# Strided deal of W and proj, a VectorE transpose of the B rows, and G through DRAM, in a LoRA and expert-mixture kernel

## The chip, the cores and the metric

The kernel runs on one core of one Trainium2 chip. The metric is device time in microseconds (us), the median of three runs. A core has five engines that run their own instruction streams and meet at semaphores: TensorE (PE in the profile, its weight loads PEld), VectorE (DVE), ScalarE (ACT), GpSimd (POOL) and SyncE (SP), which here only issues transfers. ACT and POOL issue transfers as well. All transfers of a core run on the same 16 DMA engines. Everything is in 32-bit floats.

## The reference, cut to what matters

`x` is (8, 512, 2048): 8 batches of 512 tokens. A linear layer W with bias b and a per-batch LoRA pair (A, Bm, rank 16) makes a hidden vector; a router picks one of 8 experts for each token from it; the expert's rank-16 pair adds to x.

```python
def cond(x, adapter_mapping, W, b, lora_As, lora_Bs):      # SCALING = 2
    base_out = jnp.einsum('bti,oi->bto', x, W) + b
    A, Bm = lora_As[adapter_mapping], lora_Bs[adapter_mapping]
    lora_h = jnp.einsum('bti,bir->btr', x, A)
    return base_out + jnp.einsum('btr,bro->bto', lora_h, Bm) * SCALING

def ffn(x, route_w, A, Bw):                                # E = 8, R = 16
    logits = jnp.einsum('bsd,ed->bse', x, route_w)
    topk_v, topk_idx = jax.lax.top_k(logits, 1)
    route_weight = one_hot(topk_idx[..., 0], E) * topk_v
    h = jnp.einsum('bsd,erd->bser', x, A)
    return jnp.einsum('bser,eor->bso', route_weight[..., None] * h, Bw)

out = x + ffn(cond(x, itok, W, b, lora_As, lora_Bs), route_w, A, Bw)
```

Nothing needs the 2048-wide hidden vector itself: only its 136 products with `proj` (128 expert rows and 8 router rows) are used. So the kernel folds W into proj first (C = projT W, 2048 x 136), and adds to it for each batch the product A G, where G = 2 Bm proj. Then every token tile needs one product of x with a 2048 x 136 matrix, the routing, and one product with the experts' second matrix.

## The kernel before, in words

There is no scheduler. The order of each engine's instructions is that of the program text (`tc.manual_schedule()`), and the waits between engines are placed from the tiles that they read and write.

**First stage: the fold (lines 383 to 427, about the first 77 us).** W comes in 16 chunks of 128 rows by 2048 columns (1 MB each). `load_w(oc)` (line 99) starts one transfer on SP for chunk `oc`, whose partition p holds row 128 oc + p; there are four buffers, so chunk n + 4 is started when chunk n has been copied out. `load_pj(c0, c1)` (line 94) loads the matching rows of proj, some through ACT's queue, most through SP's. `chunk_w(oc)` (line 260) copies a chunk into two half tiles in another column order, one half on ACT and one on DVE (line 274). `fold_w(oc)` (line 280) runs 16 matmuls of 128 x 136 (line 285) into six PSUM banks, which collect over all 16 chunks. A matmul in 32-bit floats shows as two instructions in the trace. `fold_w` can run a function `within` after half of its matmuls. In the last chunk it adds each bank to the adapter product of batch 0 (line 296) and copies the bank to `c` (line 297).

Between the chunks stand the adapter steps:

- `load_adapters_b` (line 157, after chunk 4) computes row numbers on DVE, gathers the 128 B rows of the 8 batches into `ad_b` with an indirect transfer of POOL (line 167) and loads the bias, which comes as 128 rows of 16 numbers, with a plain one (line 173). `load_adapters_a` (line 175, after chunk 7) gathers the A rows (line 179).
- `turn_adapters(g)` (line 313) turns the B rows with 4 TensorE transposes for each of 4 groups (line 316) and an ACT copy (line 317) into `ad_bT`.
- `fold_bias` (line 304) multiplies the bias into proj on DVE; `project_bias` and `project_adapters` (lines 321 and 326, after chunk 11) make the constant `c0b` and G, which lands in `g_sb` (line 333), one row for each of the 8 x 16 ranks.
- `spread_g(ks)` (line 335) brings 32 rows of G into all four quadrants of 32 partitions with a TensorE product against a tile of repeated identities, `eyes` (line 339), and DVE writes it out twice, each time masked by `half` (line 348), into `g4`.
- `spread_a` copies the A rows into quadrants (`ad_q`, lines 207 and 209): 20 copies on POOL after chunk 8, 4 on ACT after chunk 11.
- `first_products` (line 374) forms A G for batch 0 in pieces (line 361), two PSUM banks at a time, and copies them to `m`.

**Second stage (from line 436).** The 32 token tiles pass through `heads` (16 matmuls of x against m, line 452), `route` on DVE, `turn_heads` and `delta` (the expert product, line 546), `add_delta` and a store. x is loaded in units of two tiles by `load_x(u)` (line 116). Before a unit can be used, its quadrants are moved by 16 copies, `shuffle` (line 242, shared between POOL and ACT), and turned by DVE, `turn_x` (line 220), in 32 x 32 blocks. Units 0, 1 and 2 are loaded within the first stage (lines 405, 414 and 415); unit 0 is moved there, 10 of its copies on POOL after the A copies and 6 on ACT, and unit 1's 11 POOL copies follow.

The order around the change is, at the end of the loop's body:

```python
        if oc == 11:
            ...
            nc.sync.dma_start(out=fb, in_=ffn_b)
            load_x(1)
            load_x(2)
            project_bias()
            project_adapters()
```

Of the kernel before, what the change touches and what calls it, by code (L numbers as in the profile page):

```python
# [18 lines left out]
def kernel(  # L19
# [27 lines left out]

    nc = tc.nc  # L50
    P = 128
    Q = 32
# [21 lines left out]
    qpool = ctx.enter_context(tc.tile_pool(name="qpool", bufs=2))  # L74
    tpool = ctx.enter_context(tc.tile_pool(name="tpool", bufs=3))
    small = ctx.enter_context(tc.tile_pool(name="small", bufs=2))
    wctx = ctx.enter_context(ExitStack())
    wpool = wctx.enter_context(tc.tile_pool(name="wpool", bufs=1))
    ps_s = ctx.enter_context(tc.tile_pool(name="ps_s", bufs=2, space=bass.MemoryType.PSUM))
# [9 lines left out]

    it_i = const.tile([P, B], I32, name="it_i")  # L90
    pj = wpool.tile([P, NO, NP], F32, name="pj")
    proj_v = proj.rearrange("(c p) e -> p c e", p=P)

    def load_pj(c0, c1, eng=nc.sync):
        eng.dma_start(out=pj[:, c0:c1, :], in_=proj_v[:, c0:c1, :])  # L95
# [2 lines left out]

    def load_w(oc):
        wt = wpool.tile([P, D], F32, tag="w", bufs=4, name=f"w_{oc}")  # L100
        nc.sync.dma_start(out=wt, in_=w[ts(oc, P), :])  # L101
        w_tiles.append(wt)

    load_pj(0, 1, nc.scalar)
    load_w(0)
    load_w(1)
    load_pj(3, 5)
    load_w(2)
    load_pj(5, 8)
    load_w(3)  # L110

    x_tiles = {}
# [12 lines left out]
    make_identity(nc, ident)  # L125

    nc.scalar.copy(warm_a[:, 1:2], warm_a[:, :1])
    load_pj(1, 3, nc.scalar)
    nc.scalar.dma_start(out=it_i, in_=itok.to_broadcast([P, B]))
    pm = ps_s.tile([P, P], F32, tag="s", name="pm")  # L130
    for _ in range(14):
        nc.tensor.matmul(pm, warm, warm, start=True, stop=True)

    own_i = const.tile([P, B], I32, name="own_i")
# [15 lines left out]
    ad_b = raw[:, 0, :]  # L150
    ad_ar = raw[:, 1, :]
    fb = const.tile([P, D], F32, name="fb")
    bias_o = const.tile([P, NO], F32, name="bias_o")

    brow_f = const.tile([P, 1], F32, name="brow_f")

    def load_adapters_b():

        it_f = const.tile([P, B], F32, name="it_f")
        nc.vector.tensor_scalar(it_f, it_i, float(R), None, ALU.mult)  # L160
        row_f = const.tile([P, B], F32, name="row_f")
        nc.vector.tensor_tensor(row_f, it_f, own, ALU.add)
        nc.vector.tensor_tensor(row_f, row_f, mask, ALU.mult)
        nc.vector.tensor_reduce(brow_f, row_f, AX.X, ALU.add)
        brow_i = const.tile([P, 1], I32, name="brow_i")
        nc.vector.tensor_copy(brow_i, brow_f)  # L166
        nc.gpsimd.indirect_dma_start(  # L167
            out=ad_b,
            out_offset=None,
            in_=cond_b,  # L170
            in_offset=bass.IndirectOffsetOnAxis(ap=brow_i, axis=0),
        )
        nc.gpsimd.dma_start(out=bias_o, in_=bias)

    def load_adapters_a():

# [27 lines left out]
    def spread_a(q, k, copy):  # L204
# [3 lines left out]
        if q < 2:  # L208
            copy(dst[:, 3:], src[:, ds(JC + 2 * q, 2)])

    ad_bT = tpool.tile([P, NJ, P], F32, tag="t", name="ad_bT")

    g4 = const.tile([P, B, NP], F32, name="g4")
# [4 lines left out]
    def turn(dst, src, h):  # L218
# [7 lines left out]
    eyes = const.tile([P, NQ, Q], F32, name="eyes")  # L226
    nc.vector.tensor_reduce(
        eyes[:, 0, :], ident.rearrange("p (q c) -> p c q", c=Q), AX.X, ALU.add
    )
    nc.vector.tensor_copy(eyes[:, 1:, :], eyes[:, :1, :].to_broadcast([P, NQ - 1, Q]))  # L230

    xq_tiles = {}
    moves = [(g, i) for i in range(NQ) for g in range(NQ)]
# [26 lines left out]
    def chunk_w(oc):  # L260
        copies = (nc.scalar.copy, nc.vector.tensor_copy)
        wv = [
            wpool.tile([P, HJ, P], F32, tag=f"wv{h}", bufs=2, name=f"wv{h}_{oc}")
            for h in range(2)
        ]
        wr = w_tiles[oc].rearrange("p (i j a) -> p j i a", i=NQ, a=Q)
        for h in range(2):
            wv_tiles[oc, h] = wv[h]
            dst = wv[h].rearrange("p j (i a) -> p j i a", a=Q)

            n = HJ // 2 if oc == 0 else HJ
            for k in range(HJ // n):
                copy = copies[1 - k] if oc == 0 else copies[h]
                copy(dst[:, ts(k, n)], wr[:, ds(h * HJ + k * n, n)])  # L274
        if oc + 4 < NO:
            if oc in (0, 1):
                load_pj(8 + 4 * oc, 12 + 4 * oc)
            load_w(oc + 4)

    def fold_w(oc, within=None):  # L280
# [29 lines left out]
                    bp, pj[:, j, :], bias_o[:, j : j + 1], bp, ALU.mult, ALU.add  # L310
                )

    def turn_adapters(g):
        pt = ps_s.tile([P, 4, P], F32, tag="s", name=f"pbT_{g}")
        for k in range(4):
            nc.tensor.transpose(pt[:, k, :], ad_b[:, ts(4 * g + k, P)], ident)  # L316
        nc.scalar.copy(ad_bT[:, ts(g, 4), :], pt)

    g_sb = wpool.tile([P, NP], F32, name="g_sb")

    def project_bias():
        pb = ps_s.tile([P, NP], F32, tag="s", name="pb")
# [9 lines left out]
            )  # L332
        nc.vector.tensor_scalar(g_sb, pg, COND_SCALING, None, ALU.mult)

    def spread_g(ks):

        for k in ks:
            pq = ps_s.tile([P, NP], F32, tag="s", name=f"pq_{k}")
            nc.tensor.matmul(  # L339
                pq,  # L340
                eyes[ts(k, Q)].rearrange("p q c -> p (q c)"),
                g_sb[ts(k, Q), :],
                start=True,
                stop=True,
                tile_position=(k * Q, 0),
            )
            for h in range(2):
                nc.vector.tensor_scalar(
                    g4[:, 2 * k + h, :], pq, half[:, h : h + 1], None, ALU.mult
                )  # L350


    pieces = [(0, 3 * q, 3, q) for q in range(NQ)] + [(1, 2 * q, 2, q) for q in range(2)]
# [17 lines left out]
        part, j0, nj, _ = pieces[z]  # L371
        return (t[part][:, ds(j0, nj), :] for t in (ms[b % 2], cs))

    def first_products(some, copy=nc.vector.tensor_copy):
        banks = {
            z: ps_s.tile([P, GRP, NP], F32, tag="s", name=f"pa_{z}") for z in some
        }
        adapter_products(0, some, banks)
        for z in some:
            m, _ = place(0, z)  # L380
            copy(m, banks[z][:, : pieces[z][2], :])

    chunk_w(0)
    for oc in range(NO):
        if oc + 1 < NO:
            chunk_w(oc + 1)
        fold_w(
            oc,
            {
                13: lambda: spread_g((2, 3)),  # L390
                14: lambda: first_products((2, 3)),
            }.get(oc),
        )
# [289 lines left out]
```

## Time and profile before

| | before |
|---|---|
| median of 3 runs | 326.51 us (326.45 to 326.69) |
| the profiled execution's own time | 326.17 us |
| its span | 324.4 us |
| PE busy | 318.7 us (98%) |
| DVE, ACT, POOL busy | 230.1, 185.4, 164.9 us |
| first matmul of the fold | 7.06 us |
| first matmul of the second stage (line 452) | 77.02 us in the chain |
| DMA share, 14.87 to 68.60 us | 1.00 to 1.02 |
| HBM read, written | 54.60 MB, 33.55 MB |

The span is the time from the first to the last instruction in the trace; the 1.8 us between it and the execution's own time lie outside. The chain of waits is followed back from the last instruction, so a stretch that it gives to PE is one in which PE itself was the limit. The DMA share is the mean busy share of the 16 DMA engines. A matmul's time in the list of groups covers its pipeline; in the chain, 32 instructions of line 285 (one chunk) take 3.71 us.

### The profile page before, as it was taken

How to read it: one execution, taken by the hardware profiler on the slowest of the kernel's cores; microseconds unless marked ns; L12 is line 12 of the kernel's file. 1: busy time of each engine (PE TensorE's matmuls, PEld its weight loads, DVE VectorE, ACT ScalarE, POOL GpSimd, SP SyncE). 2: the span in 40 equal slices, each digit the busy share in tenths (PEclk: the TensorE clock that was granted, in tenths of full speed). 3: DMA queues.
4: the chain of work that ended last, by engine and by line, in shares of the span. 5: the costliest groups of instructions: out<-in, count | busy, mean ns of one | idle time of the engine just before them, and what ended most of it. 6: DMA issues, size and time to landing. Idle time of an engine off the chain costs nothing.

```text
span 324.4 us, 5611 instructions
## 1 busy us (share of the span) xinstructions
PE 318.7 (98%) x2168; PEld 252.6 (78%) x2168; DVE 230.1 (71%) x408; ACT 185.4 (57%) x230; POOL 164.9 (51%) x180
## 2 busy tenths in 40 slices
PE   8999999999999999999999999999999999999994
PEld 8999999999776777777768677767676777766762
DVE  2123183468879788887887888788787887888864
ACT  3223247527958567748764976596567758770000
POOL 1002149998967676257717771946295357710000
PEclk9999999999999999999999999999999999999999
DMA  7999999953933385859395949585876759334437
GB/s 281 365 404 421 420 418 420 421 231 120 401 129 129 131 284 235 301 233 368 153 375 229 361 165 395 184 353 165 355 255 266 270 250 358 162 162 179 174 144 250
DMA packets 15306, 88.52 MB, mean 273 GB/s; under 512 B 1696, under 2 KB 4016, under 8 KB 4912
## 3 DMA queue, kind: packets, MB, share of 16 engines
q1 hardware_dynamic: 14112, 85.45, 67.2%
q0 software_dynamic: 320, 2.11, 1.6%
q10 hardware_dynamic: 848, 0.61, 0.6%
q8 instruction: 17, 0.28, 0.4%
q14 instruction: 9, 0.07, 0.1%
HBM read 54.60 MB, written 33.55 MB: 272 GB/s over the span
## 4 chain that ended last, share of the span: by engine, by line
PE 94%; DMA 4%; SPq 0%; ACT 0%; DVE 0%; issue 0%; DVEq 0%; ACTq 0%
PE ph L452 37%; PE po L546 32%; PE pc L285 16%; PE pa L361 4%; DMA w<-in_w_dram 4%; PE pg L330 1%; PE pw L508 1%; PE pe_o L546 1%; PE pbT L316 1%; PE pe_h L546 1%; ACT wv L274 0%; DVE x L559 0%; PE pq L339 0%; PE pe_s L546 0%; SPq L101 0%; SPq L95 0%
## 5 line engine op out<-in xcount | busy, mean ns | idle before, releaser
L242 POOL COPY xq<-x 32x1024 f32<-32x1024 f32 x121 | 126.7, 1047 | 77.4 <-DMA x<-in_x_dram 26.7
L242 ACT COPY xq<-x 32x1024 f32<-32x1024 f32 x135 | 140.9, 1044 | 12.0 <-DMA x<-in_x_dram 10.0
L452 PEld LDWEIGHTS ph<-m,xT 128*128 128x128 f32 x1024 | 124.7, 190 | 20.6 <-issue 16.1
L452 PE MATMUL ph<-m,xT 128*128 128x136 f32 x1024 | 129.5, 280 | 0.0
L546 PE MATMUL po<-fb,whT 128*128 128x512 f32 x240 | 111.6, 592 | 0.0
L559 DVE TENSOR_TENSOR x<-x,po 128x1024 f32<-128x1024 f32 x60 | 72.9, 1216 | 30.6 <-PE po L546 30.4
L220 DVE STREAM_TRANSPOSE xT<-xq 128x1024 f32<-128x1024 f32 x64 | 78.9, 1236 | 2.4 <-ACT xq L242 2.4
L546 PEld LDWEIGHTS po<-fb,whT 128*128 128x128 f32 x240 | 41.7, 190 | 32.0 <-issue 32.0
L285 PE MATMUL pc<-pj,wv 128*128 128x136 f32 x512 | 61.7, 280 | 0.2 <-ACT wv L274 0.2
L285 PEld LDWEIGHTS pc<-pj,wv 128*128 128x128 f32 x512 | 60.1, 190 | 1.1 <-ACT wv L274 0.4
L513 ACT COPY whT<-pw 128x128 f32<-128x128 f32 x32 | 8.5, 267 | 54.8 <-PE pw L508 54.5
L274 DVE COPY wv<-w 128x1024 f32<-128x1024 f32 (+1 forms) x17 | 12.7, 754 | 30.8 <-PE pc L285 17.8
L274 ACT COPY wv<-w 128x1024 f32<-128x1024 f32 (+1 forms) x17 | 16.9, 998 | 28.5 <-DMA w<-in_w_dram 21.8
L504 POOL TENSOR_TENSOR m<-m,c 128x408 f32<-128x408 f32 (+1 forms) x28 | 24.5, 905 | 1.3 <-ACT m L499 0.8
L499 ACT COPY m<-pa 128x408 f32<-128x408 f32 (+1 forms) x28 | 10.4, 456 | 17.6 <-PE pa L361 17.6
L167 POOL DMA_INDIRECT raw<-in_cond_b_dram,brow_i x1 | 1.4, 1434 | 24.4 <-DVE brow_i L166 24.4
L361 PE MATMUL pa<-g,ad_q 32*128 32x136 f32 x256 | 12.7, 288 | 0.0
L361 PEld LDWEIGHTS pa<-g,ad_q 32*128 32x128 f32 x256 | 10.6, 184 | 1.3
L207 POOL COPY ad_q<-raw 32x384 f32<-32x384 f32 x12 | 6.4, 536 | 9.3 <-DMA raw<-in_cond_a_dram,arow_i 8.9
L508 PEld LDWEIGHTS pw<-ident,wh 128*128 128x128 f32 x32 | 4.5, 141 | 7.4 <-issue 7.2
L463 DVE TENSOR_TENSOR ph<-ph,c0b 128x136 f32<-128x136 f32 x32 | 9.1, 284 | 1.5 <-PE ph L452 1.5
L473 DVE TENSOR_TENSOR wh<-ph,rw 128x128 f32<-128x128 f32 x32 | 9.3, 291 | 1.1
(65 smaller groups left out, 119.7 us busy)
## 6 DMA issues: line engine op xcount, KB each, us to landing
x<-in_x_dram SPq DMA_DIRECT2D x32, 1024.0 KB, 9.3
out_dram<-x SPq DMA_DIRECT2D x30, 1024.0 KB, 4.9
w<-in_w_dram SPq DMA_DIRECT2D x16, 1024.0 KB, 11.4
out_dram<-x SPq DMA_DIRECT2D x6, 256.0 KB, 2.7
fb<-in_ffn_b_dram SPq DMA_DIRECT2D x1, 1024.0 KB, 13.7
pj<-in_proj_dram SPq DMA_DIRECT2D x2, 272.0 KB, 10.8
out_dram<-x ACTq DMA_DIRECT2D x1, 256.0 KB, 2.4
pj<-in_proj_dram SPq DMA_DIRECT2D x1, 204.0 KB, 11.3
```

The costliest lines, as they stand in the source:

```text
L220: nc.vector.transpose(dst[:, ts(h, HJ), :].rearrange("p j (g t) -> p g j t", t=Q), src.rearrange("p g (j a) -> p g j a", a=Q)[:, :, ts(h, ...
L242: copy(xq_tiles[u][ts(i, Q), :, g, :], x_tiles[u][ts(g, Q), :, ts(i, DQ)])
L274: copy(dst[:, ts(k, n)], wr[:, ds(h * HJ + k * n, n)])
L285: nc.tensor.matmul(pc[:, k, :], wv_tiles[oc, h][:, j, :], pj[:, oc, :], start=(oc == 0 and k == 0), stop=(oc == NO - 1), skip_group_check= ...
L361: nc.tensor.matmul(banks[z][:, n, :], ad_q[ts(q, Q), b // 2, 3 * part + n, :], g4[ts(q, Q), b, :], start=True, stop=True, tile_position=(q ...
L452: nc.tensor.matmul(ph_tiles[t][:, :NP], xT_tiles[t][:, j, :], m[j // JC][:, j % JC, :], start=(j == 0), stop=(j == NJ - 1),)
L463: nc.vector.tensor_tensor(ph, ph, c0b, ALU.add)
L473: nc.vector.tensor_tensor(wh.rearrange("p (e r) -> p e r", r=R), ph[:, :ER].rearrange("p (e r) -> p e r", r=R), rw.unsqueeze(2).to_broadca ...
L499: nc.scalar.copy(m, pa)
L504: nc.gpsimd.tensor_tensor(m, m, c, ALU.add)
L546: nc.tensor.matmul(part, whT_tiles[t], fb[:, ds(c, n)], start=True, stop=True)
L559: nc.vector.tensor_tensor(xs, xs, part, ALU.add)
```

## The change

The 2048 rows of W and of proj are dealt to the chunks differently: chunk c takes the rows 16p + c, p from 0 to 127, instead of 128c + p. The sum over all rows is the same. Then the B rows have to be turned so that partition p of block c holds column 16p + c, and this can be done by DVE in 32 x 32 blocks after 16 copies between quadrants: `spread_b` (12 on POOL, 4 on ACT) and `turn_b` replace `turn_adapters`. The bias has to be dealt in the same way; it is written to a DRAM tile `bias_d` in the new order and read back from there, both on POOL's queue. Proj's rows now lie together in DRAM for each partition, and its loads are grouped as 0, 1-2, 3-7 and 8-15.

G goes from `g_sb` to a DRAM tile by one transfer and from there to the quadrants by four, all on SP (`spread_g`), behind the loads of `fb` and of x unit 1 and ahead of unit 2; DVE masks it with two instructions after chunk 13 (`halve_g`). The products of `spread_g` and the tile `eyes` are gone. `first_products` runs one step later (within chunk 14, after it, and within chunk 15), and ACT does all its copies. W's first chunk comes in two transfers of half the columns each, and 8 warm-up matmuls stand at the start instead of 14.

```diff
-    proj_v = proj.rearrange("(c p) e -> p c e", p=P)
+    proj_v = proj.rearrange("(p c) e -> p c e", p=P)
+    w_v = w.rearrange("(p c) d -> c p d", p=P)
...
-        nc.sync.dma_start(out=wt, in_=w[ts(oc, P), :])
+        n = HJ if oc == 0 else NJ
+        for k in range(NJ // n):
+            dst, src = (
+                m.rearrange("p (i c) -> p i c", i=NQ)[:, :, ds(k * n * Q, n * Q)]
+                if oc == 0
+                else m
+                for m in (wt, w_v[oc])
+            )
+            nc.sync.dma_start(out=dst, in_=src)
...
-    load_pj(3, 5)
+    load_pj(1, 3)
     load_w(2)
-    load_pj(5, 8)
+    load_pj(3, 8)
     load_w(3)
...
-    load_pj(1, 3, nc.scalar)
...
-    for _ in range(14):
+    for _ in range(8):
         nc.tensor.matmul(pm, warm, warm, start=True, stop=True)
...
-        nc.gpsimd.dma_start(out=bias_o, in_=bias)
+        nc.gpsimd.dma_start(
+            out=bias_d.rearrange("(k m) c -> k m c", k=NO),
+            in_=bias.rearrange("(m c) k -> k m c", c=NO),
+        )
+        nc.gpsimd.dma_start(out=bias_o, in_=bias_d)
...
-            if oc in (0, 1):
-                load_pj(8 + 4 * oc, 12 + 4 * oc)
+            if oc == 0:
+                load_pj(8, 16)
...
-    def turn_adapters(g):
-        pt = ps_s.tile([P, 4, P], F32, tag="s", name=f"pbT_{g}")
-        for k in range(4):
-            nc.tensor.transpose(pt[:, k, :], ad_b[:, ts(4 * g + k, P)], ident)
-        nc.scalar.copy(ad_bT[:, ts(g, 4), :], pt)
+    def spread_b(ms, copy):
+        for g, i in ms:
+            copy(bq[ts(i, Q), g, :], ad_b[ts(g, Q), ts(i, DQ)])
+
+    def turn_b(h):
+        nc.vector.transpose(
+            ad_bT[:, ts(h, HJ), :].rearrange("p c (g t) -> p g c t", t=Q),
+            bq.rearrange("p g (a c) -> p g c a", c=NO)[:, :, ts(h, HJ), :],
+        )
...
-    def spread_g(ks):
...
+    def spread_g():
+        nc.sync.dma_start(out=g_dram, in_=g_sb)
+        for q in range(NQ):
+            nc.sync.dma_start(
+                out=gq[ts(q, Q)], in_=g_dram.rearrange("(k s) e -> s k e", s=Q)
+            )
+
+    def halve_g():
+        for h in range(2):
+            nc.vector.tensor_scalar(
+                g4.rearrange("p (k h) e -> p h k e", h=2)[:, h],
+                gq,
+                half[:, h : h + 1],
+                None,
+                ALU.mult,
+            )
...
-                13: lambda: spread_g((2, 3)),
-                14: lambda: first_products((2, 3)),
+                14: lambda: first_products((0, 1)),
+                15: lambda: first_products((4, 5)),
...
-        for g in {8: (0,), 9: (1, 2), 10: (3,)}.get(oc, ()):
-            turn_adapters(g)
-        if oc in (9, 10):
-            fold_bias(range(8 * (oc - 9), 8 * (oc - 8)))
         if oc == 8:
             load_x(0)
+            spread_b(moves[4:], nc.gpsimd.tensor_copy)
...
+        if oc in (8, 9):
+            spread_b(moves[2 * (oc - 8) : 2 * (oc - 7)], nc.scalar.copy)
+            fold_bias(range(8 * (oc - 8), 8 * (oc - 7)))
+        if oc == 10:
+            for h in range(2):
+                turn_b(h)
         if oc == 11:
...
             load_x(1)
-            load_x(2)
             project_bias()
             project_adapters()
+            spread_g()
+            load_x(2)
...
-        if oc == 12:
-            spread_g((0, 1))
         if oc == 13:
-            first_products((0, 1))
+            halve_g()
         if oc == 14:
-            first_products((4, 5), nc.scalar.copy)
+            first_products((2, 3))
```

More of the change, by code (lines that the diff above doesn't have):

```diff
@@ L76 @@
     small = ctx.enter_context(tc.tile_pool(name="small", bufs=2))
+    dram = ctx.enter_context(tc.tile_pool(name="dram", bufs=1, space=bass.MemoryType.DRAM))
     wctx = ctx.enter_context(ExitStack())
@@ L152 @@
     fb = const.tile([P, D], F32, name="fb")
+    bias_d = dram.tile([P, NO], F32, name="bias_d")
     bias_o = const.tile([P, NO], F32, name="bias_o")
@@ L209, in spread_a @@
             copy(dst[:, 3:], src[:, ds(JC + 2 * q, 2)])
+    bq = qpool.tile([P, 2, D], F32, tag="q", name="bq")[:, 0, :].rearrange(
+        "p (g d) -> p g d", g=NQ
+    )
     ad_bT = tpool.tile([P, NJ, P], F32, tag="t", name="ad_bT")
@@ L223, in turn @@
         )
[L226 to L230, printed above, removed]
     xq_tiles = {}
@@ L311, in fold_bias @@
                 )
-    def turn_adapters(g):
-        pt = ps_s.tile([P, 4, P], F32, tag="s", name=f"pbT_{g}")
-        for k in range(4):
-            nc.tensor.transpose(pt[:, k, :], ad_b[:, ts(4 * g + k, P)], ident)
-        nc.scalar.copy(ad_bT[:, ts(g, 4), :], pt)
+    def spread_b(ms, copy):
[6 more added lines that the diff above has]
+        )
     g_sb = wpool.tile([P, NP], F32, name="g_sb")
+    g_dram = dram.tile([P, NP], F32, name="g_dram")
+    gq = wpool.tile([P, NQ, NP], F32, name="gq")
     def project_bias():
@@ L333, in project_adapters @@
         nc.vector.tensor_scalar(g_sb, pg, COND_SCALING, None, ALU.mult)
-    def spread_g(ks):
[L337 to L345, printed above, removed]
-            )
[L347 to L350, printed above, removed]
+    def spread_g():
[3 more added lines that the diff above has]
+                out=gq[ts(q, Q)], in_=g_dram.rearrange("(k s) e -> s k e", s=Q)
+            )
+    def halve_g():
[7 more added lines that the diff above has]
+            )
     pieces = [(0, 3 * q, 3, q) for q in range(NQ)] + [(1, 2 * q, 2, q) for q in range(2)]
@@ L372, in place, with first_products @@
         return (t[part][:, ds(j0, nj), :] for t in (ms[b % 2], cs))
-    def first_products(some, copy=nc.vector.tensor_copy):
+    def first_products(some):
         banks = {
@@ L380, in first_products @@
             m, _ = place(0, z)
-            copy(m, banks[z][:, : pieces[z][2], :])
+            nc.scalar.copy(m, banks[z][:, : pieces[z][2], :])
     chunk_w(0)
```

## The prediction, made before the changed kernel ran

> **What bounds the kernel now.** I read the page first: busy shares and slices. PE is busy 98% of the span and the chain gives it 94%, so the sum is kept on PE: what PE no longer has to do is won, what makes it wait is lost.
>
> ```profile
> PE 318.7 (98%) x2168; PEld 252.6 (78%) x2168; DVE 230.1 (71%) x408; ACT 185.4 (57%) x230; POOL 164.9 (51%) x180
> ...
> PEclk9999999999999999999999999999999999999999
> ...
> PE 94%; DMA 4%; SPq 0%; ACT 0%; DVE 0%; issue 0%; DVEq 0%; ACTq 0%
> ```
>
> Then the chain in order of time, cut to the stage that the change touches:
>
> ```profile
> 2.12 11.55 DMA w<-in_w_dram
> ...
> 14.87 26.21 PE pc L285 x224
> 41.08 0.44 PE pbT L316 x4
> ...
> 54.19 3.71 PE pg L330 x32
> 57.90 3.71 PE pc L285 x32
> 61.60 0.43 PE pq L339 x4
> ...
> 66.57 0.90 PE pa L361 x12
> ```
>
> Until 14.87 the third W chunk's transfer is the limit (its landing ends the 11.55). From there PE runs without a gap: W chunks of 3.71, the transposes pbT, G (pg), its spreading (pq), the first products (pa). The second resource is seen in the table of stretches (columns: stretch and length, PE, PEld, DVE, ACT, POOL, clock, DMA share, GB/s) and in the issues (median us from issue to landing):
>
> ```profile
> 14.87:55.90 41.03, 41.03 (x355) 41.03 (x356) 14.85 (x34) 16.41 (x20) 13.81 (x24) 1.00 1.02 416
> 55.90:64.30 8.40, 8.40 (x74) 8.01 (x72) 3.13 (x7) 4.34 (x6) 8.07 (x9) 1.00 1.02 420
> ```
>
> ```profile
> w<-in_w_dram SPq DMA_DIRECT2D x16, 1024.0 KB, 11.4
> ```
>
> The DMA engines are full at 416 to 420 GB/s until after 64 us. 1 MB takes 2.5 us at that rate, but W needs 11.4 from issue to landing: some 9 us are spent in the queue behind earlier loads. That is free for loads issued early. The timeline shows how deep the queue is when G is made:
>
> ```profile
> 48.60 0.90 SPq L120 DMA_DIRECT2D x<-in_x_dram  x2
> ...
> 57.93 0.30 DVE L333 TENSOR_SCALAR g_sb<-pg 128x136 f32<-128x136 f32 x1 [3.41 <-PE pg L330]
> ...
> 66.90 12.18 POOL L242 COPY xq<-x 32x1024 f32<-32x1024 f32 x11 [0.32 <-DMA x<-in_x_dram]
> ```
>
> x unit 1 is issued at 48.6 and POOL waits for it until 66.90: a transfer put on SP's queue after unit 1 cannot land before that, though G exists at 58.2.
>
> **The change part by part** (times of the profiled execution: span 324.4, own time 326.17, 0.34 under the median 326.51).
>
> *Taken from PE.* The transposes: 0.44 + 0.87 + 0.44 = 1.75. The pq products: 2 x 0.43 = 0.86. Products of `first_products` move but stay. The chunks split by a `within` are again two (13 and 14 become 14 and 15), no difference. Sum -2.6.
>
> *The start.* The fold can begin about 1.5 earlier, since half of chunk 0 is there sooner, but the third chunk's landing decides. In the stretch 7.00 to 14.87 the DMA moved 361 GB/s instead of 416: (416 - 361)/416 x 7.87 = 1.0 lost among the small proj rows. Proj now goes in longer rows, and rows 3-4 move behind the third chunk (136 KB, 0.3); against this, chunk 0 goes in 1 KB instead of 8 KB pieces, which could cost 0.6 by the 544 B rows' lower rate. Between 0 and -1.3; I take -0.9. W's rows keep their 8 KB, so I cost the deal itself at nothing; if rows 128 KB apart read slower, the queue only gets longer, which is priced below. The 8 warm-up products (424 ns each: 5.94 / 14) end near 4.5, before the fold's first product near 5.5: a cold start there hides under the wait for the second and third chunk.
>
> So far -3.5: the second stage would start at 73.5 instead of 77.02, and the point where PE first needs `g4`, inside chunk 14, lies at 13.97 (third chunk starts) + 10 x 3.71 + 3.94 (pb, pg) + 2 x 3.71 + 2.28 = 64.7.
>
> *G through DRAM.* G is in `g_sb` near 55.3. Its write is issued on SP then, but stands behind `fb` and x unit 1 in the queue. The bytes ahead of it are the same as before (only unit 2 is moved behind it), so it lands just after unit 1: 66.9 + 0.3 = 67.2. Only then SP may issue the four reads (they wait for the write): 4 issues of 0.43 (the row of a proj load with as many pieces), the last starting at 68.5, landing 2.4 later (the shortest landing on the page, ACT's 256 KB store) = 70.9. `halve_g`: two instructions of 128 x 544; DVE's copy of 1024 takes 0.69, so 0.4 to 0.6 each, 1.0 in all: 71.9. PE waits from 64.7 to 71.9: +7.2. Bounds: if the DMA lost nothing anywhere, 25.2 MB (16.8 W, 1.1 proj, 2.1 A and B rows, 1.0 fb, 4.2 x) at 420 GB/s from 2.5 us end at 62.5, the chain gives 68.5 and PE waits 4; if the queue ends 3 later, it waits 10. Behind SP's wait stand x units 2 to 4: unit 2 is issued near 69 on an empty DMA and takes 2 x 2.5 + 2.4, so 76; POOL took it up at 80.17 before. On DVE the copy of chunk 15's second half and `turn_x` stand behind `halve_g`; they need 0.69 + 2.4 and are used 5 us after PE resumes. ACT's copies of pa, then its last two moves of unit 0, also come after the wait (to 76), still ahead of a second stage at 81 or later.
>
> *The clock after a wait.* The rows: warm-up products 424 ns for 128 columns, chunk products 3.71 / 16 = 232 ns for 136, while PEclk reads 9 in both. TensorE started at half speed and took until about 7 us to be fast. By the Trainium skill's "TensorE: Matmul & The Clock Gate" (What's actually happening) an idle window of some 3.4 us puts it back to half speed until a busy window has passed. No wait that long is in this trace. By the trace alone the wait costs 7.2; by the rule a slow stretch of 3.4 to 6 us follows, which loses half: 1.7 to 3.0. I take 2.3, since 7.2 holds a whole window wherever it begins.
>
> *The bias and POOL.* Here the skill speaks against the change: "DMA: Bandwidth & Descriptors" (Rules for kernel authors) says that a strided last dimension becomes one descriptor per element, so 2048 pieces of 4 B. POOL then waits for that write before it issues `bias_o` and the A rows. Nearest row: the old bias load on the same queue landed 10.7 after its issue (27.33), behind the B rows. With 2 us for the pieces POOL is free near 40, not 34.7. Upper end: ACT's 544 B proj rows went one for one with W's 8 KB rows, about 0.3 each per engine; 128 pieces per engine at that pace are 38 us. The page's packets of up to 64 descriptors (SWDGE vs HWDGE vs iDMA) would make it two or three such turns. I take 2 us and keep 38. Then A is issued at 40.5 (landing 9.8 later, 50.3), 12 copies of B take 12 x 0.64 (between 0.536 for 384 and 1.047 for 1024) to 49.2, DVE turns twice (2 x 1.24) to 51.7: pg half a microsecond late. 20 A copies (6.4 + 3.8) end at 60.5, unit 0's 10 (11.6) at 72.1, unit 1's 11 (12.2) at 84.3. All of it hides under the wait for G. If that cover is gone, unit 1, which was needed by 77.02 + 6.5 and had 1.2 of slack, is 84.3 - (73.5 + 7.7) = 3.1 late, and most of the gain is lost there.
>
> *Sum:* -3.5 + 7.2 + 2.3 = +6.0. Span 330.4, time 332.2, on the median 332.5.
>
> **The rivals.**
>
> 1. *The wait without the clock penalty:* -3.5 + 7.2 = +3.7, 330.2. For it: no such restart is in the trace. Both ends of the queue estimate with it: 327 to 333.
>
> 2. *Faster: G arrives in time.* If the DMA's backlog is gone when G is made, or the write doesn't stand behind unit 1, write and reads take 2.4 + 1.3 + 2.4 + 1.0 = 7.1 from 55.3: 62.4, before 64.7. Deciding point: the reads landed by 63.7. Then the gain is 3.5, less up to 3.1 by POOL: 323.0 to 326.1. For it: the order leaves 9 us between G and its use. Against: 1.02 of DMA share up to 64 us and unit 1's 18 us from issue to use.
>
> 3. *POOL becomes the bound:* the 2048 pieces take long to generate or to pass. From a release of POOL at 46 on, unit 1 is late even with the wait; at 40 + 36 the A rows land at 86, unit 0 is moved by 108 and the second stage starts near 111: 360. For a few us more, 334 to 340. For it: rows of 0.3 per small piece; against: the POOL queue's bias load, which shows no such cost.
>
> 4. *The change doesn't do what it says:* the transposes' 1.75 leave PE for certain (16 instructions fewer), so I see no case of this beyond rival 2's loss.
>
> **How the numbers follow.** Wait with clock penalty 0.45, wait without 0.20, POOL bound 0.17, G in time 0.18, of which 0.05 within the bound of no change because POOL eats the gain. A difference of 0.2% (0.65 us) is about what a measurement of this kernel can tell from none. Slower 0.82, same 0.05, faster 0.13. The likeliest case by itself: 329 to 335.5. For 8 in 10 the range leaves out the long POOL cases (some 0.10) and the better part of rival 2 (some 0.09): 324.5 to 337.5.
>
> **What would show it.** Right: the chain gains a DMA piece gq<-g_dram and DVE g between two PE pc pieces of chunk 14, with some 7 us of PE idle before the first pa; g_dram's landing 10 us or more after its issue; the chunk after it at 0.4 us a product. pbT and pq gone; third chunk's first product near 14.0. Wrong: gq landed before 63.7, or PE's gap before pg instead (POOL's B copies), or pa without a gap. If the reads land in time and the time still rises, the POOL row of unit 1 (L242's successor) ending after 83 names rival 3.

## The result, and the profile after

| | before | after |
|---|---|---|
| median | 326.48 us (325.76 to 326.69, 6 runs) | 346.08 us (342.51 to 351.27, 6 runs) |
| ratio to before | | 1.059 (95% interval 1.0543 to 1.0638) |
| profiled execution, own time and span | 326.17, 324.4 us | 342.51, 340.7 us |
| third W chunk's first matmul | 14.87 us | 15.9 us |
| first matmul of the second stage | 77.02 us | 92.93 us |
| from there to the end of the span | 247.4 us | 247.8 us |

Ratios and their intervals leave out runs more than 1.5% above the fastest of their kernel, which are one of the changed kernel's (351.27) and, further below, two of the four of `e2_pieces_only`; a median is over all runs.

The change is slower by 5.9%: 19.6 us in the medians and 16.3 us between the two profiled executions. The changed kernel's profiled execution is the shortest of its runs, so the 3.6 us by which its median is longer have no trace. 15.9 of the 16.3 arise ahead of the second stage; after it the two kernels take the same time. From here on, times are of the profiled executions.

The page of the changed kernel, busy shares, granted clock by slices of 8.5 us, and the chain by engine:

```profile
PE 321.7 (94%) x2132; PEld 254.9 (75%) x2132; DVE 230.3 (68%) x398; ACT 187.5 (55%) x234; POOL 173.3 (51%) x193
...
PEclk9999969879999999999999999999999999999999
...
PE 71%; DMA 15%; POOL 8%; issue 2%; DVE 1%; ACT 1%; SPq 0%; DVEq 0%; POOLq 0%
```

PE has 36 instructions fewer, and yet is busy 3 us longer: the clock row falls to 6 in slice 6 and to 8 and 7 in slices 8 and 9. Before, the chain gave PE 94%; now 23% of it lie on DMA and POOL. The chain in order of time, first 96 us (start, length, what):

```profile
27.28 19.16 DMA bias_d<-in_bias_dram
...
47.60 11.04 DMA raw<-in_cond_a_dram,arow_i
...
58.68 0.72 POOL bq L328
```

A transfer of 8 KB, the bias on its way to `bias_d`, took 19.16 us; only then could POOL issue `bias_o` and the A rows, and POOL's B copies waited for the A rows. The waits behind it in the list of waits (engine, line, releaser: us in total, times, longest):

```profile
POOL bq L328 <- DMA raw<-in_cond_a_dram,arow_i: 9.4, 1, 9.4
...
DVE bp L320 <- DMA bias_o<-bias_d: 7.4, 1, 7.4
```

The stretches of one microsecond (PE, PEld, DVE, ACT, POOL busy, granted clock, DMA share, GB/s) show that the bias didn't only wait, it stopped the other transfers too:

```profile
36.00:37.00 1.00, 1.00 (x11) 1.00 (x10) 0.00 (x0) 0.00 (x0) 0.00 (x0) 1.00 6.35 192
37.00:38.00 1.00, 1.00 (x11) 1.00 (x11) 0.00 (x0) 0.00 (x0) 0.00 (x0) 1.00 0.41 17
...
40.00:41.00 1.00, 1.00 (x11) 1.00 (x10) 0.00 (x0) 0.00 (x0) 0.00 (x0) 1.00 0.00 0
...
45.00:46.00 1.00, 0.38 (x1) 0.38 (x2) 0.24 (x1) 1.00 (x2) 0.00 (x0) 0.50 1.25 287
```

The share of 6.35 is time of W's own rows, booked where they began. The single packets of the trace show it: a W row of 8 KB takes 0.31 us (median from 30 to 35 us), but 16 of those that began between 36.0 and 37.7, as many as there are DMA engines, took 5.85 to 7.67. Just ahead of them and among them, from 35.4 to 37.6, 32 packets of 256 B start on POOL's queue, together the 8 KB of the pieces, each booked with 0.08 us. So W's open rows show the hold, and the pieces' own records don't. From 37 to 44 us next to nothing moved, with W chunks outstanding. PE ran out of W at 42.09, as its timeline shows (start, length, instructions, idle before and releaser):

```profile
12.17 29.92 PE L298 MATMUL pc<-pj,wv 128*128 128x136 f32 x256 [0.31 <-ACT wv L287]
45.62 8.62 PE L298 MATMUL pc<-pj,wv 128*128 128x136 f32 x48 [3.53 <-ACT wv L287]
56.35 3.97 PE L298 MATMUL pc<-pj,wv 128*128 128x136 f32 x32 [2.10 <-DVE wv L287]
...
68.36 5.65 PE L349 MATMUL pg<-pj,ad_bT 128*128 128x136 f32 x32 [5.36 <-DVE ad_bT L331]
73.85 9.66 PE L298 MATMUL pc<-pj,wv 128*128 128x136 f32 x82
83.44 0.96 PE L381 MATMUL pa<-g,ad_q 32*128 32x136 f32 x12
```

The books of the 15.9, in us: PE work removed -2.6; the start +1.0; idle for W 3.5; 48 instructions at the slow clock in 8.62 instead of 5.57, 3.05; idle 2.1 and 0.3 because DVE stood at `bp` for the bias, with W copies behind it; idle 5.4 before pg, and pg in 5.65 instead of 3.87, 1.8; idle before the second stage 1.0, because POOL moved unit 0 until 88.2 and DVE turned it ahead of the sums for `m`. Together 15.6.

What isn't there is the wait for G. Between the last `pc` group and the first `pa` (83.44) PE has no gap. SP's timeline:

```profile
61.52 0.90 SPq L132 DMA_DIRECT2D x<-in_x_dram  x2
74.38 0.33 SPq L356 DMA_DIRECT2D g_dram<-g_sb  x1
76.48 2.69 SPq L358 DMA_DIRECT2D gq<-g_dram  x4
```

G's write was issued 12.9 us after x unit 1, the queue was empty, and the write landed in 2.1 us.

### The profile page after: what moved, and what is told of

It reads as the page before. It is cut to its first block, busy times and chain, and to the rows that moved or that the text cites. A ratio compares the mean times of both kernels' runs of the same rounds, so it can differ in the third digit from the quotient of the medians.

```text
span 340.7 us, 5554 instructions
## 1 busy us (share of the span) xinstructions
PE 321.7 (94%) x2132; PEld 254.9 (75%) x2132; DVE 230.3 (68%) x398; ACT 187.5 (55%) x234; POOL 173.3 (51%) x193
## 3 DMA queue, kind: packets, MB, share of 16 engines
q1 hardware_dynamic: 14448, 85.94, 67.1%
## 4 chain that ended last, share of the span: by engine, by line
PE 71%; DMA 15%; POOL 8%; issue 2%; DVE 1%; ACT 1%; SPq 0%; DVEq 0%; POOLq 0%
PE ph L474 35%; PE po L568 30%; DMA w<-in_w_dram 6%; DMA bias_d<-in_bias_dram 6%; DMA raw<-in_cond_a_dram,arow_i 3%; POOL xq L255 3%; PE pa L381 3%; POOL bq L328 2%; POOL ad_q L224 2%; PE pw L530 1%; PE pe_o L568 1%; POOL ad_q L226 1%; PE pe_h L568 1%; ACT c L310 0%; DVE xT L240 0%
## 5 line engine op out<-in xcount | busy, mean ns | idle before, releaser
L298 PE MATMUL pc<-pj,wv 128*128 128x136 f32 x512 | 66.8, 295 | 6.9 <-ACT wv L287 3.8
L298 PEld LDWEIGHTS pc<-pj,wv 128*128 128x128 f32 x512 | 65.1, 203 | 8.4 <-ACT wv L287 4.2
L287 DVE COPY wv<-w 128x1024 f32<-128x1024 f32 (+1 forms) x17 | 13.4, 789 | 37.5 <-DMA w<-in_w_dram 25.3
L328 POOL COPY bq<-raw 32x512 f32<-32x512 f32 x12 | 7.8, 650 | 9.9 <-DMA raw<-in_cond_a_dram,arow_i 9.4
L381 PE MATMUL pa<-g,ad_q 32*128 32x136 f32 x256 | 12.7, 288 | 0.0
L349 PE MATMUL pg<-pj,ad_bT 128*128 128x136 f32 x32 | 5.6, 354 | 5.4 <-DVE ad_bT L331 5.4
```

The source lines that it names most:

```text
L298: nc.tensor.matmul(pc[:, k, :], wv_tiles[oc, h][:, j, :], pj[:, oc, :], start=(oc == 0 and k == 0), stop=(oc == NO - 1), skip_group_check= ...
L328: copy(bq[ts(i, Q), g, :], ad_b[ts(g, Q), ts(i, DQ)])
L381: nc.tensor.matmul(banks[z][:, n, :], ad_q[ts(q, Q), b // 2, 3 * part + n, :], g4[ts(q, Q), b, :], start=True, stop=True, tile_position=(q ...
```

## The experiments

### Two halves of the theory, each alone

Theory: without the pieces, the prediction's account holds (G's write stands in the queue behind x unit 1, and the clock falls after the wait); the pieces of the bias add the rest, by holding the DMA engines. Three kernels test it; before took 326.24 us beside them.

`e1_bias_plain`, the changed kernel with the bias loaded as before, so that it is not dealt as W's rows are:

```diff
-        nc.gpsimd.dma_start(
-            out=bias_d.rearrange("(k m) c -> k m c", k=NO),
-            in_=bias.rearrange("(m c) k -> k m c", c=NO),
-        )
-        nc.gpsimd.dma_start(out=bias_o, in_=bias_d)
+        nc.gpsimd.dma_start(out=bias_o, in_=bias)
```

> The changed kernel with one edit: the bias comes with the old plain load (128 rows of 16), so its values stand at the wrong outputs; everything else is as changed. Theory P (the 2048 pieces of 4 B hold the DMA engines and POOL, and that is where the time went): most of the 19.6 us come back, 325 to 329 us; chunk 9 lands by 37 us, no PE gap at 42 us, bias landed by 40. Theory Q (the prediction's: G's write stands behind x unit 1 and PE waits for it): 331 to 333 us, with a PE gap of 4 to 8 us before the first pa. A late pg of 2 us can come in both, since in the changed kernel POOL's B copies waited for the A rows.

Measured: 332.89 us (331.60 to 334.47), ratio 1.020 [1.016, 1.0241]. 13.2 of the 19.6 us between the medians are gone. Its PE timeline and SP's:

```profile
55.15 3.94 PE L343 MATMUL pg<-pj,ad_bT 128*128 128x136 f32 x32 [1.83 <-DVE ad_bT L325]
...
72.72 1.73 PE L375 MATMUL pa<-g,ad_q 32*128 32x136 f32 x12 [4.13 <-DVE g L358]
74.38 3.54 PE L292 MATMUL pc<-pj,wv 128*128 128x136 f32 x14
```

```profile
59.46 0.33 SPq L350 DMA_DIRECT2D g_dram<-g_sb  x1
67.44 1.75 SPq L352 DMA_DIRECT2D gq<-g_dram  x4
```

Now the wait for G is there: the write, issued at 59.46, lets the reads go only at 67.44, and PE waits 4.13 us before `pa`. After the wait 12 `pa` instructions take 1.73 us (0.96 elsewhere) and 14 `pc` instructions 3.54 (1.89). So the rest of the change, that is W's new rows, the first chunk in two transfers, the B turn and G's detour, costs 6.65 us together.

`e2_pieces_only`, before with the pieces transfer added after its own bias load, and nobody reading what it writes:

```diff
         nc.gpsimd.dma_start(out=bias_o, in_=bias)
+        nc.gpsimd.dma_start(
+            out=bias_d.rearrange("(k m) c -> k m c", k=NO),
+            in_=bias.rearrange("(m c) k -> k m c", c=NO),
+        )
```

> The kernel before plus the one transfer of 2048 pieces of 4 B to DRAM, issued by POOL after the bias load; nobody reads it or waits for it. Theory P: the DMA engines are held some 6 us near 36 to 42 us all the same, chunk 9 lands after 43, PE waits 3 to 4 us and runs at half clock for some 6 us after it: 332 to 335 us. If it is only POOL's wait for the landing that costs: 326.5 us.

Measured: 335.98 us (330.83 to 337.93), ratio 1.0195 [1.0128, 1.0262]. The profiled execution is the longest of these four (337.93), so its sizes are upper ones. PE waits 9.34 us for W:

```profile
55.41 5.67 PE L291 MATMUL pc<-pj,wv 128*128 128x136 f32 x32 [9.34 <-ACT wv L280]
```

POOL waits for the A rows, here and, in the second fence, before:

```profile
60.53 0.49 POOL L213 COPY ad_q<-raw 32x384 f32<-32x384 f32 x1 [24.80 <-DMA raw<-in_cond_a_dram,arow_i]
```

```profile
44.59 0.55 POOL L207 COPY ad_q<-raw 32x384 f32<-32x384 f32 x1 [8.85 <-DMA raw<-in_cond_a_dram,arow_i]
```

No instruction waits for the pieces here, so the loss is the hold on the DMA engines alone. Again 16 W rows, begun between 36.8 and 38.7, took 6.2 to 8.5 us.

`e3_g_dram_only`, before with only G's way through DRAM (the `eyes` tile and `pq` products out, the write, four reads and `halve_g` in, as in the change, the order of `first_products` with them):

```diff
...
-            spread_g((0, 1))
+            spread_g()           # after project_adapters, ahead of load_x(2)
...
+    nc.sync.dma_start(out=g_dram, in_=g_sb)
+    for q in range(NQ):
+        nc.sync.dma_start(out=gq[ts(q, Q)], in_=g_dram.rearrange("(k s) e -> s k e", s=Q))
```

> The kernel before with only the G part of the change: G through DRAM behind x unit 1, masked by two VectorE instructions, first products one step later; B rows turned by TensorE and the bias as before. Theory Q: g_sb near 58, the write lands only at 67 or later, the reads near 71, PE waits 3 to 5 us before the first pa and then runs at half clock for some us: 330 to 333 us. Theory P (G's way costs nothing): 0.9 us fewer on PE, 325.5 us.

Measured: 332.32 us (332.18 to 332.48), ratio 1.0183 [1.0166, 1.02]: almost all of what the change costs without the pieces. SP's and PE's timelines, and the stretch with the clock (0.50):

```profile
57.83 0.33 SPq L334 DMA_DIRECT2D g_dram<-g_sb  x1
67.06 1.75 SPq L336 DMA_DIRECT2D gq<-g_dram  x4
```

```profile
71.60 1.73 PE L359 MATMUL pa<-g,ad_q 32*128 32x136 f32 x12 [4.64 <-DVE g L342]
73.26 3.54 PE L280 MATMUL pc<-pj,wv 128*128 128x136 f32 x14
76.73 1.60 PE L359 MATMUL pa<-g,ad_q 32*128 32x136 f32 x12
```

```profile
72.00:74.00 2.00, 2.00 (x15) 1.75 (x14) 2.00 (x2) 0.67 (x2) 1.92 (x3) 0.50 0.99 401
```

The write of 68 KB lands 9.2 us after its issue, just after x unit 1 (POOL takes unit 1 up at 66.91). The three groups at the slow clock take 6.87 us instead of 3.81: the clock costs 3.1 us after a wait of 4.64.

### G on another queue

`e8_g_on_act_queue` is the kernel above with the write and the reads issued by ACT.

```diff
-        nc.sync.dma_start(out=g_dram, in_=g_sb)
+        nc.scalar.dma_start(out=g_dram, in_=g_sb)
...
-            nc.sync.dma_start(
+            nc.scalar.dma_start(
```

> e3_g_dram_only with one edit: G's write and four reads are issued on ACT's queue instead of SP's. Theory Q (the wait is the stand behind x unit 1 in SP's queue): the write lands 2 to 4 us after its issue instead of 9, the reads by 65, no PE gap before the first pa, 325.4 to 326.5 us (the upper end if ACT, which waits for the write, is late with its half of chunk 13). If the DMA engines' backlog holds any queue: 331 to 333 us.

Measured: 334.43 us (333.64 to 335.65), ratio 1.0265 [1.0234, 1.0297]. A miss: it is slower than on SP's queue. ACT's timeline, PE's, and a stretch of two microseconds:

```profile
58.02 0.34 ACTq L334 DMA_DIRECT2D g_dram<-g_sb  x1
64.64 1.81 ACTq L336 DMA_DIRECT2D gq<-g_dram  x4
66.54 1.04 ACT L269 COPY wv<-w 128x1024 f32<-128x1024 f32 x1 [12.88 <-issue]
```

```profile
67.64 7.92 PE L280 MATMUL pc<-pj,wv 128*128 128x136 f32 x50 [6.28 <-ACT wv L269]
```

```profile
62.00:64.00 2.00, 0.00 (x0) 0.00 (x0) 0.20 (x1) 0.00 (x0) 1.96 (x2) 1.00 1.01 419
```

On a queue with nothing else in it the write still took 6.6 us: the DMA engines are full (share 1.01), and the other queue's loads are served beside it. That is 2.6 less than on SP. But ACT stands in its own issue until then, and its W copy stands behind: PE waits 6.28 us for W, earlier than it would have waited for G. The reads go beside x unit 2, which SP no longer holds back, and land 8.1 us after issue instead of 2.0. So both full engines and queue order delay G; here the other queue moved the wait and didn't remove it. Whether a queue whose engine has nothing behind it would do better was not tried.

### How the hold depends on the number and the size of the pieces

`e12_pieces_half` has the first half of the unused transfer (1024 pieces of 4 B); `e13_pieces_16B` moves the same 8 KB in 512 pieces of 16 B.

```diff
-            out=bias_d.rearrange("(k m) c -> k m c", k=NO),
-            in_=bias.rearrange("(m c) k -> k m c", c=NO),
+            out=bias_d.rearrange("(k m) c -> k m c", k=NO)[:8],       # e12
+            in_=bias.rearrange("(m c) k -> k m c", c=NO)[:8],
+            out=bias_d.rearrange("p (a b) -> (p a) b", b=4).rearrange("(a p) b -> a p b", a=4),   # e13
+            in_=bias.rearrange("p (a b) -> a p b", b=4),
```

> Before, with the first half of the unused pieces transfer: 1024 pieces of 4 B in place of 2048. Theory N (each piece costs its share of the hold): the DMA engines are held some 3 us in place of 6, which the queue's 1.4 us of slack in W's landings covers partly: +1 to +3.5, 327.5 to 330, against 335.98 with all. Rival T (the hold is per transfer, whatever its pieces): 334 to 336.

Measured: 332.41 us (331.39 to 333.08), ratio 1.0184 [1.0161, 1.0207].

> Before, with an unused transfer of the same 8 KB in 512 pieces of 16 B (the value order is another, nobody reads it). Theory N (the cost goes with the number of pieces): a quarter of the hold, 1.5 us, mostly within the slack of W's landings: 326.5 to 328. Rival B (the cost goes with the bytes or with the transfer): 334 to 336.

Measured: 326.07 us (325.68 to 326.63), ratio 1.0001 [0.9991, 1.001]. POOL's first A copy, with half the pieces and with 16 B pieces, and between them PE's wait with half the pieces:

```profile
53.66 0.88 POOL L213 COPY ad_q<-raw 32x384 f32<-32x384 f32 x1 [17.86 <-DMA raw<-in_cond_a_dram,arow_i]
```

```profile
50.24 6.52 PE L291 MATMUL pc<-pj,wv 128*128 128x136 f32 x32 [4.13 <-ACT wv L280]
```

```profile
45.67 0.95 POOL L213 COPY ad_q<-raw 32x384 f32<-32x384 f32 x1 [10.35 <-DMA raw<-in_cond_a_dram,arow_i]
```

Against 44.59 before, the A rows are 1.1 us late with 512 pieces of 16 B, 9.1 with 1024 of 4 B and 15.9 with 2048 of 4 B (the last in e2's longest run). Bytes are not what costs, since the 16 B kernel moves all 8 KB. Half the pieces cost more than I expected: a wait of 4.13 us for W was again paid twice, by the idle time and by the clock (32 `pc` instructions in 6.52 instead of 3.87).

The single packets show why half the pieces do not cost half. In `e12` 8 W rows that began between 36.8 and 37.6 took 6.7 to 8.3 us, where in `e2` 16 took 6.2 to 8.5, and six rows after them took 3.5 to 6.9. So at first half as many rows were held, each for as long, and a chunk is complete only with all its rows. In `e13` no W row took longer than 1.1 us. (Each of the three transfers leaves 32 small packets in the trace, those of `e12` and `e13` with more bytes than they move, so the packets don't tell the pieces apart.) Whether the number or the size of the pieces decides stays open, since 512 pieces of 4 B were not tried; so does what is slow in a 4 B piece.

### The start

`e4_first_chunk_two` is before with chunk 0 in two transfers and 8 warm-up products; `e5_two_late_itok` is that with the token map's load (128 pieces of 32 B) issued after chunk 0; `e6_late_itok_only` is before with that last edit alone.

```diff
-        nc.sync.dma_start(out=wt, in_=w[ts(oc, P), :])       # e4, e5: chunk 0 as two halves of 1 KB pieces
...
+            nc.sync.dma_start(out=dst, in_=src)              # for k in range(NJ // n), as in the change
...
-    nc.scalar.dma_start(out=it_i, in_=itok.to_broadcast([P, B]))   # e5, e6: moved into the loop, oc == 0
```

> The kernel before with only the first W chunk in two transfers of half the columns (1 KB pieces) and 8 warm-up products for 14. If the 1 KB pieces are what made the second chunk late in the changed kernel (copied at 11.07 instead of 8.76 us): the fold's second chunk again starts near 12 and the time is 327 to 328 us. If it was the strided deal or the proj loads: the second chunk by 9 us and 325.5 to 326.5 us.

Measured: 328.91 us (328.04 to 329.18), ratio 1.007 [1.0053, 1.0087]: the split, with fewer warm-up products, is a loss. PE's timeline and a stretch:

```profile
5.46 2.12 PE L293 MATMUL pc<-pj,wv 128*128 128x136 f32 x16 [0.91 <-DVE wv L282]
10.84 11.44 PE L293 MATMUL pc<-pj,wv 128*128 128x136 f32 x82 [3.25 <-DVE wv L282]
```

```profile
6.00:7.00 1.00, 1.00 (x11) 1.00 (x10) 0.00 (x0) 0.00 (x0) 0.00 (x0) 1.00 0.58 123
```

The first half comes 1.6 us earlier than before, at the price of the second: 123 GB/s in 6 to 7 us, a wait of 3.25, and the slow clock behind it.

> e4_first_chunk_two with one edit: the load of the token map (128 pieces of 32 B, ACT's queue) is issued after the fold's first chunk instead of at the start. Theory H (small pieces hold the DMA engines, and these 128 made the hole in which the first chunk's second half was late): the second half lands by 8 us instead of 10.35, the PE gap of 3.25 us before it shrinks below 1.5, 326 to 327 us. If the 1 KB pieces alone are slow: no change, 328.9 us.

Measured: 326.25 us (326.02 to 327.07), ratio 1.0003 [0.9994, 1.0012]. The hole in the first chunk is gone: the second half is copied at 7.81 instead of 10.35.

> The kernel before with only the token map's load issued later. Theory H: the DMA's hole at 8 to 10 us goes, the third chunk's first product starts near 13.7 instead of 14.87, 325.2 us. Otherwise 326.2 us.

Measured: 325.72 us (325.08 to 326.22, 20 runs), ratio 0.9981 [0.9975, 0.9988]. The fold now runs from 6.60 without the gap at 14.87, until W's fifth chunk is the limit. The hole has moved behind the token map's new place (before, 8 to 10 us: 253 GB/s; here 14 to 16):

```profile
14.00:16.00 2.00, 2.00 (x20) 2.00 (x19) 0.62 (x2) 0.65 (x1) 0.00 (x0) 1.00 0.60 172
```

So in both places the token map's small pieces make a hole in the DMA, and two half chunks gain nothing of their own. The gain of 0.2% is that of the 20 runs; the profiled one is the slowest of them (326.22), and its pg starts at 54.08, before's at 54.03.

### The deal and the B turn without the detours

`e9_deal_only`: before with W and proj dealt and DVE turning the B rows, B copies half on ACT and half on DVE out of a tile of their own (in the change, A and B rows share the tile `raw`, and POOL has 12 of the 16), G on PE as before. The bias is turned on PE, written to DRAM in rows of 512 B and read back, both on ACT's queue:

```diff
+            nc.tensor.transpose(pbias, bias_r, ident)
+            nc.scalar.copy(bias_t, pbias)
+            nc.scalar.dma_start(out=bias_d, in_=bias_t)
+            ...
+            nc.scalar.dma_start(out=bias_o, in_=bias_d.rearrange("m (a c) -> (m a) c", c=NO))
```

> The strided deal and the VectorE turn of the B rows alone, with the pieces and POOL's load taken out: chunk 0 in one transfer, 14 warm-up products, G through TensorE as before; the 16 B copies go half to ACT and half to VectorE instead of mostly to POOL; the bias is turned by one TensorE transpose and goes through DRAM in 512 B rows on ACT's queue. Expected: the transposes' 1.75 us minus 0.1 for the bias are won, 324.4 to 325 us, if DVE and ACT carry the copies between the chunks without making PE wait. If the strided deal itself slowed W's loads, the chunks' landings shift and it is 326 or more.

Measured: 346.31 us (345.24 to 347.27), ratio 1.0624 [1.0591, 1.0657], as bad as the change, and none of the theories had that. DVE's timeline, then PE's:

```profile
54.27 0.29 DVE L315 TENSOR_SCALAR bp<-pj,bias_o 128x136 f32<-128x136 f32 x1 [2.44 <-DMA bias_o<-bias_d]
54.59 7.47 DVE L317 SCALAR_TENSOR_TENSOR bp<-pj,bias_o,bp 128x136 f32<-128x136 f32 x7
...
63.46 7.33 DVE L317 SCALAR_TENSOR_TENSOR bp<-pj,bias_o,bp 128x136 f32<-128x136 f32 x8
```

```profile
70.94 0.79 PE L335 MATMUL pb<-bp,warm 128*128 128x136 f32 x2 [17.73 <-DVE bp L317]
```

The bias landed at 54.27, so its products, which in before run from 41.73, fell into POOL's copies of x. The 15 with an accumulator took 1.0 us each there (0.39 and 0.50 in before). PE, which has `pb` ahead of `pg` in its order, waited 17.73 us for a product that the second stage needs much later.

`e14_deal_turn` is that kernel (B rows in their own tile, copied by ACT and DVE), but takes the bias as an input already laid out by the deal (a reordering on the host, no arithmetic), so that one plain load stays, and moves `project_bias` by two chunks:

```diff
-        "bias": np.asarray(L0_cond_b).reshape(-1, 128).T,
+        "bias": np.asarray(L0_cond_b).reshape(128, -1),
...
-            project_bias()          # after chunk 11
+            project_bias()          # after chunk 13, behind first_products((0, 1))
...
+            fold_bias({8: range(3), 9: range(3, 8), 11: range(8, NO)}[oc])
```

> Before, with W and proj dealt and VectorE turning the B rows; B copies half on ScalarE and half on VectorE, issued ahead of x unit 0's copies; the bias is handed over already laid out for the deal, so that one plain load of 128 rows of 64 B remains; G stays on PE; the bias product later by two chunks. Theory D (the deal itself costs nothing; what was lost in the deal-only run was the bias on its way through DRAM, which let VectorE start its 15 bias products only at 54.3 us and at 1 us each beside POOL's copies): PE gives up 1.75 us of transposes, the start loses up to 1.0, no wait before pg: -1.75 to -0.5, 324.8 to 326.0. Rival R (rows 128 KB apart slow W's stream, or VectorE's two turns come late beside POOL): a wait before pg of 2 us or more and the clock's restart, 329 or more.

Measured: 325.29 us (325.05 to 325.46), ratio 0.9969 [0.9957, 0.9981]. PE's timeline:

```profile
10.98 41.19 PE L290 MATMUL pc<-pj,wv 128*128 128x136 f32 x352 [0.67 <-ACT wv L279]
52.02 3.87 PE L339 MATMUL pg<-pj,ad_bT 128*128 128x136 f32 x32
...
75.82 6.65 PE L465 MATMUL ph<-m,xT 128*128 128x136 f32 x56
```

From 10.98 to pg PE has no wait, and pg starts 2.2 us ahead of before's 54.19: 1.75 of transposes, 0.23 of `pb`, which comes later, and 0.2 of the start. 0.67 are given back before `pb`, and the second stage starts 1.2 us earlier. Theory D held: the deal costs W's stream nothing (422 GB/s from 11 to 36 us; before moved 416 from 14.87 to 55.90), and rival R's wait doesn't occur.

`e15_deal_turn_late_itok` adds the late token map.

> The deal-and-turn kernel with the token map's load issued after W chunk 0, as in the run that had only this. If the two gains add: 0.6 less than the deal-and-turn run, 324.2 to 325.4, ahead of before by 0.3 to 0.7%. If the third W chunk sets the start in any case: equal to the deal-and-turn run.

Measured: 325.31 us (325.06 to 325.42), ratio 0.9965 [0.9952, 0.9979], the same as without it. The gains don't add: pg starts at 52.02 in both, since W's stream and not the fold's first start sets it. `e14` and `e15` are both faster than before, by 0.3%, and than after. The two ratios' intervals nearly cover each other, so they can't be ranked.

## Why the prediction was wrong, and where it was right

**The sign and the forecast's mechanism.** Slower was right. The wait for G behind x unit 1 in SP's queue and the slow clock behind it are real, but not in the kernel that ran: without the pieces (e1) the time is 332.89 against 332.5 predicted; with them PE was so late that the queue had emptied, and no wait for G came. The forecast was right for a kernel that the change was not.

**The step that failed: "I take 2 us and keep 38"**, for the 2048 pieces of 4 B. The old load's 10.7 us from issue to landing became 19.2 and not 12.7, so the term of 2 us measured 8.5. And the text put at nothing what the pieces do to everybody else: from 37 to 44 us the DMA engines moved next to nothing. I bounded the pieces as a delay of POOL, priced by the pace of proj rows on ACT's queue, when the resource they take is the one that the same text had shown to be full. The "two or three such turns" fit the record, in which 32 packets are two for each of 16 engines. Their price was wrong: the W rows open beside them took 5.85 to 7.67 us. e2 shows that the hold alone, waited for by nobody, costs about 2%; e1 that taking the pieces out of the change gives back 13.2 us. That what e1 gives back beyond e2's loss lies in the waits for the bias and the A rows is my reading of the books; no run has the same waits without the hold.

**Rival 3** had the right transfer and a time of 334 to 340 "For a few us more", with a chance of 0.17, and the range left its long cases out. Three of the prediction's own signs came: the gap before pg, pa without a gap, and POOL's row of unit 1 ending after 83 (its moves of unit 0 alone last until 88.2).

**POOL "free near 40".** It was 46.7 when POOL issued `bias_o`, and 47.6 for the A rows (prediction 40.5). Their landing took 11.0 instead of 9.8.

**"12 copies of B ... to 49.2 ... pg half a microsecond late".** The copies took 0.69 us each (11 in 7.61), near the 0.64 predicted, but from the second on they start only when the A rows have landed, which the text had at 50.3: by its own numbers the copies would have ended near 57.5, and turned B would have been several microseconds late. I read the copies' work and not their waits. That wait is 9.4 us in after and 7.3 in e1, where it costs PE 1.83. Why POOL's copies stand for rows that they don't read isn't shown; ACT's B copies, out of the same tile, ran ahead of that landing (until 50.7, A rows at 58.6). DVE's two turns took 1.85 each, not 1.24.

**The start, -0.9.** It was +1.0. The estimate took chunk 0's half as early and free. e4 and e5 show that the second half is late as long as the token map's 32 B pieces run beside it. W's deal at nothing was right (e14).

**G's way, term by term.** Write landing "67.2": 67.4 in e1, 67.1 in e3. Reads 2.4: 2.2 and 2.0. `halve_g` 1.0 for two: 2.5 in e1, 2.2 in e3 and 1.9 in after, but PE goes on after the first of the two. The end of the wait, put at 71.9, came at 71.60 in e3 and 72.72 in e1. Wait +7.2: 4.64 in e3 and 4.13 in e1, because PE needed `g4` at 67.0 and 68.6 and not at 64.7: the gains of 3.5 ahead of it were not there (e3 has only 0.86 of them; in e1 the start and the wait of 1.83 for B used them up). That e1 meets the forecast to 0.4 us is for this reason less luck than it seems: the end of the wait hangs on the write's landing, so what was wrong ahead of it changed the length of the wait and not its end. One sum doesn't come out: the lower bound of that end, 62.5 and the 5.0 from unit 1's landing (66.9) to 71.9, is 67.5 and a wait of 3, where the text has 68.5 and 4.

**The clock.** The prediction weighed the trace (nothing) against the Trainium skill's "TensorE: Matmul & The Clock Gate" (What's actually happening), and took 2.3 of 1.7 to 3.0. e3 agrees in kind, with a granted clock of 0.50 in the stretch from 72 to 74 us, and shows 3.1 after 4.64 us of idle: the clock stayed low for 6.8 us, more than the 3.4 to 6 assumed. The changed kernel paid it twice, after waits of 3.53 and 5.36 (3.05 and 1.8). The wait of 2.10 before 56.35 brought none: 32 instructions in 3.97.

## What to carry to other kernels

Look at the pieces of a transfer and not only at its bytes: beside full DMA engines 2048 pieces of 4 B cost everyone who waits for a load, including those that have nothing to do with them, 1024 still did, and the same 8 KB in 512 pieces of 16 B cost nothing. When a small result is sent through DRAM in the middle of a load stream, ask what has been issued ahead of it and what the issuing engine has behind it; in e8 another queue only moved the wait. And when an operation is moved to another engine, list what that engine's order makes it wait for and who runs beside it, not only how long it takes.

## What the runs showed of the hardware that I had not expected

- Small pieces stop large ones on other queues. Beside the 4 B pieces 16 W rows of 8 KB took 5.85 to 7.67 us instead of 0.31, and all loads together fell to 0 GB/s for 4 us (38 to 42) and stayed under 70 for 7, where they had run at 418 until 35 us.
- A write on an empty queue is not quick while the engines are full: 68 KB took 6.6 us on ACT's, 9.2 on SP's behind x, and 2.1 when nothing else moved.
- Idle PE time can be paid twice: waits of 3.25 us (e4) and more were followed by a granted clock of 0.50, for up to 6.5 us of work (e3), and waits of 2.1 and less were not. The clock fell between 2.0 us (after, before pg) and 4.3 us (e3) after PE's last product, so these traces give no sharp limit.
- DVE's 128 x 136 product with an accumulator took 0.39 us in one place and 1.0 in another (e9), in the latter beside POOL's copies of x. That POOL is the cause wasn't tested by itself.
